# The start of an attention block with a gated feed-forward: GpSimd's order, and k of the first sequence by single tiles

## The chip, the cores and the metric

The kernel runs on one core of one Trainium2 chip. The core has five engines that run side by side and wait for each other through semaphores: PE (TensorE, matmuls, with a sequencer of its own for weight loads, PEld), DVE (VectorE), ACT (ScalarE), POOL (GpSimd) and SP (SyncE, which here only starts DMAs). DMAs are started from SP's queue or from ACT's, and sixteen DMA engines move the data.

The metric is the device time of one execution in microseconds; less is better. Three executions of the kernel before took 610.42, 611.47 and 612.76 us, so its median is 611.47 us. A further execution was profiled; it took 612.91 us.

## The reference

x has 8 sequences of 512 tokens with 256 features. Everything is float32 with a tight tolerance.

```python
xn = layernorm(x)                       # over the 256 features, eps 1e-5
# attention: 16 heads of 16, q and k rotated, a window of 250 tokens, causal
q, k, v = split(xn @ in_proj_w.T)       # in_proj_w: 768 x 256
q, k = rope(q), rope(k)
scores = (q . k) * 16 ** -0.5, masked to 0 <= t - s < 250
s = (softmax(scores) @ v) @ out_proj_w.T
# feed-forward with weights +1 or -1, from boolean matrices
h = s0 * (concat(xn, -xn) @ sign(k0))   # 512 -> 1024
h = s1 * ((2 * relu(h)) @ sign(k1))     # 1024 -> 1024
h = s2 * ((2 * relu(h)) @ sign(k2))     # 1024 -> 256
out = x + s * silu(h)
```

## The kernel before

**Tiles.** Features lie on the 128 partitions in the products: x is brought to x^T (2 chunks of 128 features by 512 tokens), and every matmul has up to 512 tokens as its columns. The feed-forward splits each activation into a high part in fp16 and a low part in fp32r (`h1h` and `h1l`, `h2h` and `h2l`) and multiplies each with its own copy of the weights (`w1h`, `w1l`); a group of 128 features is one PSUM tile `h_ps`, whose high part ACT takes out and whose low part DVE takes out after it. A PSUM tile is free for the next group only after both. Three such tiles rotate in the pool `ps_m`; the pool `ps_s` has two, which serve the first sequence's transposes, then q, then v, and later the scores.

**Order.** Nothing is scheduled by the hardware. `run` takes a list of pieces, each with a hand-written place (a number, about microseconds from the start of the first sequence's feed-forward; 42 for each sequence) and a cost, and emits them in the order of places; a piece may return follow-ups with delays in the same clock. The order in which pieces are emitted is the order in each engine's queue, and each engine works strictly through its queue. Sequence b+1 is prepared while sequence b runs, so PE has work almost all the time; the first sequence has nobody ahead of it.

**The first sequence.** Its four tiles of 128 tokens are loaded (`load_x`, L111), two from SP and two from ACT, and ACT also loads the scales `s_sb` and then the weights of k, q and v. `stats` (L245) takes mean and variance of each tile on DVE (`bn_stats`, `bn_aggr`), adds EPS (L256) and has GpSimd raise it to the power -0.5 (L257); for the first sequence this is done for two tiles at once (`n = 2`). `norm` (L309) scales a tile on DVE, `turn_x` (L315) transposes it on PE and has ACT copy it to `xT`. `project` (L375) makes k and q as two parts of 128 features, `a` and `b`; for k of the first sequence by halves of 256 tokens. Then, for k and for q alike:

- `both` multiplies the parts with cosine and sine on DVE (L404: `m_ka`, `m_kb`, `m_qa`, `m_qb`). `m_kb` and `m_qb` are one and the same buffer.
- `rotate` (L421, the work in L425) adds and subtracts them on GpSimd, two instructions of 128x512.
- `split_hi` (L439) casts the result on ACT (`kh`, `qh`; one buffer) and stores it to DRAM, `split_lo` (L445) takes the rest on DVE (L449) and stores that. q is stored twice, in two orders. `stack` (L452) loads k, q and the second q back, turned, for the scores.

`hi_after` and `lo_after` (L401) are the places of the two splits, counted from the second part's product.

**GpSimd and ACT beside it.** The weights of the second layer are made from booleans in blocks of 128 output features (`make_w1`, L188, L192 on ACT and L194 on DVE or GpSimd), placed by the list at L998: `w1l` 0 and 1 at -20 and -19 on GpSimd, `w1h` 0 and 1 at -17 and -16 on ACT. Places below zero come ahead of the first sequence's feed-forward, and so ahead of the rotations of its k and q.

Of the kernel before, what the change touches and what calls it, by code (L numbers as in the profile page):

```python
# [34 lines left out]
def tile_attention_times_gated_ffn(  # L35
# [42 lines left out]
    nc = tc.nc  # L78
    P = 128
    B, T, E = x.shape  # L80
    H = HEADS
    D = E // H
    NT = T // P
# [25 lines left out]
    xs = {}  # L109

    def load_x(b, t):  # L111
        xs[b, t] = xpool.tile([P, E], F32, tag=f"x{t}", name=f"x_{b}_{t}")
        queue = nc.scalar if b == 0 and t >= NT // 2 else nc.sync
        queue.dma_start(xs[b, t], x[b, ts(t, P), :])

    raw = ctx.enter_context(ExitStack())
    raw_pool = raw.enter_context(tc.tile_pool(name="raw", bufs=1))
    s_sb = const.tile([P, 5], F32, name="s_sb")
# [6 lines left out]
    kb2 = raw_pool.tile([P, NF1, E], U8, name="kb2")  # L125
    for t in range(NT):
        load_x(0, t)
    nc.scalar.dma_start(s_sb, s)
    for n in (1, 0, 2):
        nc.scalar.dma_start(  # L130
            wqkv_sb[:, :, ts(n, E)], w_qkv[:, ts(n, E)].rearrange("(c p) f -> p c f", p=P)
        )
# [109 lines left out]
            follow(at, g())  # L242


    def stats(b):  # L245
        st = states[b] = {}

        n = 2 if b == 0 else NT
        mv = st["mv"] = moments[:, b % 2, : 3 * NT].rearrange("p (i t) -> p t i", t=NT)
        for t in range(NT):  # L250
            bn = small.tile([P, 6], F32, tag="bn", name=f"bn_{b}_{t}")
            nc.vector.bn_stats(bn, xs[b, t])
            nc.vector.bn_aggr(mv[:, t, 1:3], bn)
            if (t + 1) % n == 0:
                part = mv[:, t + 1 - n : t + 1, 0]
                nc.vector.tensor_scalar(part, mv[:, t + 1 - n : t + 1, 2], EPS, None, ALU.add)  # L256
                nc.gpsimd.tensor_tensor(part, part, minus_half[:, :n], ALU.pow)  # L257
        if b > 0:
            enough(b)

# [48 lines left out]
    def norm(b, t):  # L309
        mv, xn = states[b]["mv"], xs[b, t]  # L310
        nc.vector.tensor_scalar(
            xn, xn, mv[:, t, 1:2], mv[:, t, 0:1], ALU.subtract, ALU.mult
        )

    def turn_x(b, t, plain=False):  # L315

        st = states[b]
        xn = xs.pop((b, t))
        if t == 0:
            st["xT"] = one.tile([P, EC, T], F32, tag="xT", name=f"xT_{b}")  # L320
            if plain:
                st["xp"] = one.tile([P, EC, T], F32, tag="xl", name=f"xp_{b}")
            else:
                for p, dt in (("h", F16), ("l", F32R)):
                    st["x" + p] = one.tile([P, EC, T], dt, tag="x" + p, name=f"x{p}_{b}")
        if not plain and t == 2:
            pt = ps_o.tile([P, T], F32, tag="po", name=f"xnT_ps_{b}_{t}")
            pt = pt[:, : EC * P].rearrange("p (c q) -> p c q", c=EC)
        elif not plain and t < 2:

            pt = ps_s.tile([P, 2, T], F32, tag="sc", name=f"xnT_ps_{b}_{t}")
            pt = pt[:, 0, : EC * P].rearrange("p (c q) -> p c q", c=EC)
        else:
            pt = ps_m.tile([P, EC, P], F32, tag="mm", name=f"xnT_ps_{b}_{t}")
        for c in range(EC):
            nc.tensor.transpose(pt[:, c, :], xn[:, ts(c, P)], ident)
        if plain:
            nc.vector.tensor_copy(st["xT"][:, :, ts(t, P)], pt)
            nc.scalar.mul(st["xp"][:, :, ts(t, P)], pt, sgnx)
            return  # L340
        hi, lo = (st["x" + p][:, :, ts(t, P)] for p in "hl")


        nc.scalar.copy(st["xT"][:, :, ts(t, P)], pt)
        st["parts", t] = [
            lambda: nc.scalar.mul(hi, pt, sgnx),
            lambda: nc.vector.scalar_tensor_tensor(lo, pt, sgnx, hi, ALU.mult, ALU.subtract),
        ]
        if t + 1 == NT:
            first_parts(0, 1)  # L350

    def first_parts(*tiles):
        for t in tiles:
            for f in states[0].pop(("parts", t)):
                f()
# [16 lines left out]
        return [(0.0, lambda: nc.scalar.copy(v_pad[:, t, :, 0:3:2, :], v))]  # L372


    def project(b, what, part, half=None):  # L375

        st = states[b]
        col = E * "qk".index(what) + P * "ab".index(part)
        if b == 0 and what == "q":
            ps = ps_s.tile([P, 2, T], F32, tag="sc", name=f"{what}{part}_ps_{b}")[:, 0]  # L380
        elif half == 1:
            ps = st.pop(part)
        else:
            ps = ps_m.tile([P, T], F32, tag="mm", name=f"{what}{part}_ps_{b}")
            st[part] = ps
        for cols in [slice(0, T)] if half is None else [ts(half, T // 2)]:
            for c in range(EC):
                nc.tensor.matmul(
                    ps[:, cols], wqkv_sb[:, c, ds(col, P)], st["xT"][:, c, cols],
                    start=(c == 0), stop=(c == EC - 1),  # L390
                )
        if half == 0:
            return

        m = turned.tile(
            [P, 2, T], F32, tag=f"m{part}", name=f"m_{what}{part}_{b}",
            bufs=2 if part == "a" else 1,
        )
        st[what, part] = m

        hi_after, lo_after = (4.0, 5.1) if b else (4.5, 5.7) if what == "k" else (5, 6.2)  # L401

        def times(i):
            nc.vector.tensor_tensor(  # L404
                m[:, i], ps, rope_sb[:, i if part == "a" else 1 - i], ALU.mult
            )

        def both():
            times(0)
            times(1)  # L410
            if part == "b":
                return [
                    (1.4, lambda: rotate(b, what)),
                    (hi_after, lambda: split_hi(b, what)),
                    (lo_after, lambda: split_lo(b, what)),
                ]


        return [(1.5 if b == 0 and what + part == "qb" else 0.0, both)]
# [40 lines left out]
    def prepare(b, plain=False):  # L460

        if b == 0 or plain:
            at = dict(stats=-40, norm=-38, x=-36, k=0, q=3, v=9.2)
            dp, dv = 1.5, 1.5
        else:

            at = dict(load=9, stats=9, down=10.5, over=12, norm=16.8, k=21.8, q=24.8, v=SEQ + 0.6)
            if b == 1:
                at.update(load=18.65, stats=15, down=18, over=18.7, norm=24.8, k=26.6, q=28.4)
            dp, dv = 1.5, 1.0  # L470
            at = {n: SEQ * (b - 1) + f for n, f in at.items()}
        out = [(at["stats"], 0, lambda: stats(b))]
        if "over" in at:
            out += [
                (at["load"], 0, lambda: load_xT(b)), (at["down"], 0, lambda: lay_down(b)),
                (at["over"], 0, lambda: lay_over(b)),
                (at["norm"], 0, lambda: norm_turned(b, 0)),
                (at["norm"] + 1.2, 0, lambda: norm_turned(b, 1)),
            ]
        for t in range(NT):  # L480
            if "over" not in at:
                out += [
                    (at["norm"] + t, 0, lambda t=t: norm(b, t)),
                    (at["x"] + t, 0.25, lambda t=t: turn_x(b, t, plain)),
                ]
            out.append((at["v"] + dv * t, 0.87, lambda t=t: project_v(b, t)))
        for what in "kq":
            for n, part in enumerate("ab"):
                if b == 0 and what == "k" and not plain:

                    out += [
                        (-34.3 if n == 0 else -32.95, 0.87, lambda p=part: project(b, "k", p, 0)),
                        (at["k"] + dp * n, 0.87, lambda p=part: project(b, "k", p, 1)),
                    ]
                else:
                    out.append((
                        at[what] + dp * n, 1.75, lambda w=what, p=part: project(b, w, p),
                    ))
        return out
# [496 lines left out]
            (-32.9 if c == 0 else -32.6, 0, lambda c=c: make_w0l(c)),  # L996
        ]
    for w, f, at, engine in (  # L998
        ("l", 0, -20, nc.gpsimd), ("l", 1, -19, nc.gpsimd), ("l", 2, 5.1, nc.gpsimd),
        ("h", 0, -17, nc.scalar), ("h", 1, -16, nc.scalar), ("h", 2, 5.2, nc.gpsimd),  # L1000
        ("l", 3, 11.8, nc.gpsimd), ("l", 4, 11.9, nc.gpsimd), ("l", 5, 12.0, nc.gpsimd),
        ("l", 6, 19.3, nc.gpsimd), ("l", 7, 19.4, nc.gpsimd), ("h", 3, 15.2, nc.scalar),
        ("h", 4, 17.0, nc.scalar), ("h", 5, 18.7, nc.scalar), ("h", 6, 20.4, nc.scalar),
        ("h", 7, 22.2, nc.scalar),
    ):
        everything.append((at, 0, lambda f=f, w=w, e=engine: make_w1(f, w, e)))
    for b in range(B):
# [4 lines left out]
        for t in range(NT):  # L1012
            if b + 1 < B:
                at = SEQ * b + 1.5 if b else 2.0
# [133 lines left out]
```

## Time and profile before

| | |
|---|---|
| median of three runs | 611.47 us |
| the profiled execution, its whole time | 612.91 us |
| its span, first to last instruction | 611.2 us |
| mean granted TensorE clock | 0.991 |
| PE busy | 596.9 us, 98% of the span |
| DVE / ACT / POOL busy | 384.2 / 295.1 / 308.0 us |

PE is the engine that sets the time. Its row is busy in all slices of the page but the first and the last, so what matters is where it stands still or runs at a lower clock. The profile gives, for each instruction, start, length and what ended the idle time before it; "[1.65 <-ACT v_pad L372]" behind an instruction says that its engine stood idle for 1.65 us until ACT's instruction at line 372 was done. `h_ps<-h1h,w1h_sb` means that the tile `h_ps` is written from `h1h` and `w1h_sb`. "PEclk" is the clock granted to TensorE as a share of full speed.

### The profile page before, as it was taken

The numbers are of one execution on the slowest core, as the hardware profiler recorded it, in microseconds if no ns is written. First come the engines' busy times: TensorE is split into PE (matmuls) and PEld (weight loads), VectorE is DVE, ScalarE is ACT, GpSimd is POOL, SyncE is SP. The second block draws the span as 40 slices with busy tenths as digits, with TensorE's granted clock in tenths as the row PEclk, the third lists the DMA queues.
The fourth block names the chain that finished last, engine by engine and source line by source line (L and its number), as shares of the span: only waits on it lengthen the run. The fifth ranks groups of instructions, "written<-read, shape, count | busy, mean of one in ns | idle before, by whom it ended". The sixth has DMA issues, their size and how long they took to land. (4 is left out here: it accounts for less than half of the span.)

```text
span 611.2 us, 11176 instructions
## 1 busy us (share of the span) xinstructions
PE 596.9 (98%) x4492; PEld 367.7 (60%) x4492; DVE 384.2 (63%) x606; ACT 295.1 (48%) x414; POOL 308.0 (50%) x368
## 2 busy tenths in 40 slices
PE   7899999999999999999999999999999999999994
PEld 5465565556665556555566566655565556667783
DVE  6654736556675584665856658566676557654774
ACT  4576654435544545545354454543554445555421
POOL 2855542346524665336634357245572446627642
PEclk9799999999999999999999999999999999999998
DMA  9371732216322263314333252432533216212201
GB/s 286 144 242 53 276 122 86 87 70 229 117 87 87 97 215 104 120 55 180 131 104 122 79 218 73 148 112 80 207 101 123 89 69 241 70 54 75 83 1 41
DMA packets 38061, 74.51 MB, mean 122 GB/s; under 512 B 5360, under 2 KB 13040, under 8 KB 38000
## 3 DMA queue, kind: packets, MB, share of 16 engines
q1 hardware_dynamic: 35568, 71.48, 34.0%
q10 hardware_dynamic: 2432, 2.23, 1.1%
q8 instruction: 37, 0.61, 0.4%
q14 instruction: 24, 0.20, 0.1%
HBM read 44.30 MB, written 29.39 MB: 121 GB/s over the span
## 5 line engine op out<-in xcount | busy, mean ns | idle before, releaser
L752 ACT ACTIVATE p<-sc 128x1024 f32<-128x1024 f32 (+2 forms) x144 | 138.3, 1013 | 75.5 <-PE sc L733 45.8
L768 POOL TENSOR_SCALAR_AFFINE_SELECT p<-p 128x512 f32<-128x512 f32 x128 | 91.1, 718 | 126.6 <-ACT p L752 126.5
L518 PE MATMUL h_ps<-h1l,w1l_sb 128*128 128x512 f32 (+1 forms) x576 | 146.2, 396 | 0.0
L518 PE MATMUL h_ps<-h1h,w1h_sb 128*128 128x512 f16 (+1 forms) x576 | 123.1, 356 | 0.0
L518 PEld LDWEIGHTS h_ps<-h1l,w1l_sb 128*128 128x128 f32 x576 | 100.2, 188 | 29.5 <-issue 9.2
L529 ACT ACTIVATE h2h<-h_ps 128x512 f16<-128x512 f32 (+1 forms) x72 | 39.5, 548 | 112.3 <-PE h_ps L518 112.3
L518 PEld LDWEIGHTS <-w1h_sb 128*128 128x128 f16 x576 | 51.2, 98 | 58.7 <-issue 17.3
L775 POOL TENSOR_SCALAR_AFFINE_SELECT p<-p 128x512 f32<-128x512 f32 (+1 forms) x96 | 49.7, 517 | 70.9 <-ACT p L752 67.4
L807 PE MATMUL po<-p,v_pad 128*32 128x378 f32 (+4 forms) x1216 | 76.7, 372 | 0.1
L633 DVE RECIPROCAL den<-den 128x256 f32<-128x256 f32 (+1 forms) x32 | 52.5, 1644 | 24.9 <-POOL den L628 24.9
L527 DVE SCALAR_TENSOR_TENSOR h2l<-h_ps,h2h 128x512 fp32r<-128x512 f32 (+1 forms) x72 | 43.7, 608 | 30.9 <-ACT h2h L529 30.9
L733 PEld LDWEIGHTS sc<-q,k 32*128 32x128 f32 x1216 | 44.0, 184 | 29.4 <-issue 21.5
L527 DVE SCALAR_TENSOR_TENSOR h1l<-h_ps,h1h 128x512 fp32r<-128x512 f32 x64 | 42.8, 680 | 29.4 <-ACT h1h L529 29.4
L884 DVE RECIPROCAL S<-S 128x128 f32<-128x128 f32 x64 | 57.5, 920 | 0.1
L733 PE MATMUL sc<-q,k 32*128 32x378 f32 (+4 forms) x1216 | 57.4, 306 | 0.1
L518 PE MATMUL h_ps<-xl,w0l_sb 128*128 128x512 f32 x128 | 53.7, 501 | 0.0
L807 PEld LDWEIGHTS po<-p,v_pad 128*32 128x32 f32 x1216 | 31.7, 109 | 28.7 <-issue 16.6
L529 ACT ACTIVATE h1h<-h_ps 128x512 f16<-128x512 f32 x64 | 38.1, 598 | 22.1 <-PE h_ps L518 22.1
L518 PE MATMUL h_ps<-xh,w0h_sb 128*128 128x512 f16 x128 | 39.8, 393 | 1.1 <-DVE h1l L527 1.1
L301 DVE TENSOR_TENSOR xT<-xT,of_all 128x512 f32<-128x512 f32 x28 | 22.7, 815 | 26.4 <-DMA of_all<-d 26.0
L572 PE MATMUL z_ps<-h2l,w2l_sb 128*128 128x512 f32 (+1 forms) x144 | 36.1, 391 | 0.2 <-DVE h2l L527 0.2
L365 PE MATMUL v_ps<-wqkv_sb,xT 128*128 128x256 f32 x128 | 33.8, 387 | 1.6 <-ACT v_pad L372 1.6
(101 smaller groups left out, 721.5 us busy)
## 6 DMA issues: line engine op xcount, KB each, us to landing
q<-dq SPq DMA_DIRECT2D x64, 256.0 KB, 3.4
dq<-qh SPq DMA_DIRECT2D x16, 512.0 KB, 3.2
dq<-m_qa SPq DMA_DIRECT2D x16, 512.0 KB, 5.5
k<-dk SPq DMA_DIRECT2D x32, 256.0 KB, 2.7
dk<-kh SPq DMA_DIRECT2D x8, 512.0 KB, 3.6
dk<-m_ka SPq DMA_DIRECT2D x8, 512.0 KB, 2.6
x<-in_x_dram SPq DMA_DIRECT2D x30, 128.0 KB, 2.8
xT<-in_x_t_dram SPq DMA_DIRECT2D x7, 512.0 KB, 5.3
```

The lines of the kernel that those rows point to most:

```text
L365: nc.tensor.matmul(v.rearrange("p n s d -> p (n s d)"), st["xT"][:, c, ts(t, P)], wqkv_sb[:, c, 2 * E :], start=(c == 0), stop=(c == EC - 1),)
L518: nc.tensor.matmul(ph, w[p][:, c, ts(f, P)], st[src + p][:, c, cols], start=(k == 0), stop=(k == n - 1),)
L527: nc.vector.scalar_tensor_tensor(lo, ph, 0.0, hi, ALU.max, ALU.subtract)
L529: high = lambda: nc.scalar.activation(hi, ph, AF.Relu)
L572: nc.tensor.matmul(pz, w2[p][:, c, ts(f, P)], st["h2" + p][:, c, cols], start=(c == 0 and p == "h"), stop=(c == NF1 - 1 and p == "l"),)
L633: nc.vector.reciprocal(part, part)
L733: nc.tensor.matmul(sc[r // 2][:, r % 2, ds(off, n)], st["k0", g][row, ts(j, P)], st[f"q{turn}", g][row, ds(j * P + first, n)], start=(turn ...
L752: nc.scalar.activation(p[:, 2 * half : 2 * half + 2, :n], sc[half][:, :, :n], AF.Exp, scale=D ** -0.5,)
L768: nc.gpsimd.affine_select(out=block, in_=block, compare_op=ALU.is_ge, fill=0.0, base=0, pattern=[[0, 4], [1, P]], channel_multiplier=-1,)
L775: nc.gpsimd.affine_select(out=block, in_=block, compare_op=ALU.is_ge, fill=0.0, base=-1, pattern=[[0, 4], [-1, beyond]], channel_multiplier=1,
L807: nc.tensor.matmul(po[32 * r : 32 * r + 32, ds(j * P + first, n)], v_columns(j, g, r), p_[:, r, ds(off, n)], start=(j == 0), stop=(done an ...
L884: nc.vector.reciprocal(part, part)
```

## The change

Four things change, all of them at the start of the kernel.

- Loads: all four tiles of x go to SP's queue, and ACT's queue begins with the weights of k; `s_sb` comes behind them.
- Statistics of the first sequence: by single tiles (`n = 1`), and `stats` itself calls `norm` of a tile once the next tile's statistics are queued.
- k of the first sequence: by tiles of 128 tokens, each right behind the transpose that it needs; the transposes have new places.
- GpSimd and ACT: `w1l` 0 and 1 move from -20 and -19 to 4.6 and 4.65, so GpSimd's queue has the rotation of k, these two blocks, the rotation of q, and then `w1l` 2 and `w1h` 2, which were ahead of q's rotation. `w1h` 1 moves on ACT from ahead of the first evacuation to behind the second (behind `kh` and `h1h` of group 1, ahead of the first copy of v). The splits have new places: the low part of k comes behind the low part `h1l` of group 1 instead of ahead of it, and the low part of q ahead of `h1l` of group 5 instead of behind it.

A branch that computes everything anew when a value is out of range uses the same functions; it isn't entered with these inputs.

```diff
     def load_x(b, t):
         xs[b, t] = xpool.tile([P, E], F32, tag=f"x{t}", name=f"x_{b}_{t}")
-        queue = nc.scalar if b == 0 and t >= NT // 2 else nc.sync
-        queue.dma_start(xs[b, t], x[b, ts(t, P), :])
+        nc.sync.dma_start(xs[b, t], x[b, ts(t, P), :])
...
-    nc.scalar.dma_start(s_sb, s)
     for n in (1, 0, 2):
+        if n == 0:
+            nc.scalar.dma_start(s_sb, s)
         nc.scalar.dma_start(
...
-    def stats(b):
+    def stats(b, plain=False):
...
-        n = 2 if b == 0 else NT
+        n = 1 if b == 0 and not plain else NT
...
                 nc.gpsimd.tensor_tensor(part, part, minus_half[:, :n], ALU.pow)
+            if n == 1 and t > 0:
+                norm(b, t - 1)
+        if n == 1:
+            norm(b, NT - 1)
...
-        for cols in [slice(0, T)] if half is None else [ts(half, T // 2)]:
+        for cols in [slice(0, T) if tile_ is None else ts(tile_, P)]:
             for c in range(EC):
                 nc.tensor.matmul(
                     ps[:, cols], wqkv_sb[:, c, ds(col, P)], st["xT"][:, c, cols],
...
-        if half == 0:
+        if tile_ is not None and tile_ + 1 < NT:
             return
...
-        hi_after, lo_after = (4.0, 5.1) if b else (4.5, 5.7) if what == "k" else (5, 6.2)
+        hi_after, lo_after = (4.0, 5.1) if b else (5.0, 6.2) if what == "k" else (4.6, 5.4)
...
-                    (at["x"] + t, 0.25, lambda t=t: turn_x(b, t, plain)),
-                ]
+                if b > 0 or plain:
+                    out.append((at["norm"] + t, 0, lambda t=t: norm(b, t)))
+                out.append((
+                    at["x"] + t if plain else (-36, -35, -34.3, -33.3)[t], 0.25,
+                    lambda t=t: turn_x(b, t, plain),
+                ))
...
-                    out += [
-                        (-34.3 if n == 0 else -32.95, 0.87, lambda p=part: project(b, "k", p, 0)),
-                        (at["k"] + dp * n, 0.87, lambda p=part: project(b, "k", p, 1)),
-                    ]
+                    for t, places in enumerate(((-35.5, -34.9), (-34.6, -33.6), (-0.9, -0.6), (0, 1.5))):
+                        out.append((
+                            places[n], 0.43, lambda p=part, t=t: project(b, "k", p, t),
+                        ))
...
-        ("l", 0, -20, nc.gpsimd), ("l", 1, -19, nc.gpsimd), ("l", 2, 5.1, nc.gpsimd),
-        ("h", 0, -17, nc.scalar), ("h", 1, -16, nc.scalar), ("h", 2, 5.2, nc.gpsimd),
+        ("l", 0, 4.6, nc.gpsimd), ("l", 1, 4.65, nc.gpsimd), ("l", 2, 10.2, nc.gpsimd),
+        ("h", 0, -17, nc.scalar), ("h", 1, 8.6, nc.scalar), ("h", 2, 10.3, nc.gpsimd),
```

More of the change, by code (lines that the diff above doesn't have):

```diff
@@ L372, in project_v, with project @@
         return [(0.0, lambda: nc.scalar.copy(v_pad[:, t, :, 0:3:2, :], v))]
-    def project(b, what, part, half=None):
+    def project(b, what, part, tile_=None):
         st = states[b]
@@ L380, in project @@
             ps = ps_s.tile([P, 2, T], F32, tag="sc", name=f"{what}{part}_ps_{b}")[:, 0]
-        elif half == 1:
-            ps = st.pop(part)
+        elif tile_:
+            ps = st[part]
         else:
@@ L471, in prepare @@
             at = {n: SEQ * (b - 1) + f for n, f in at.items()}
-        out = [(at["stats"], 0, lambda: stats(b))]
+        out = [(at["stats"], 0, lambda: stats(b, plain))]
         if "over" in at:
@@ L481, in prepare @@
             if "over" not in at:
-                out += [
-                    (at["norm"] + t, 0, lambda t=t: norm(b, t)),
-                    (at["x"] + t, 0.25, lambda t=t: turn_x(b, t, plain)),
-                ]
+                if b > 0 or plain:
[4 more added lines that the diff above has]
+                ))
             out.append((at["v"] + dv * t, 0.87, lambda t=t: project_v(b, t)))
@@ L489, in prepare @@
                 if b == 0 and what == "k" and not plain:
-                    out += [
-                        (-34.3 if n == 0 else -32.95, 0.87, lambda p=part: project(b, "k", p, 0)),
-                        (at["k"] + dp * n, 0.87, lambda p=part: project(b, "k", p, 1)),
-                    ]
+                    for t, places in enumerate(((-35.5, -34.9), (-34.6, -33.6), (-0.9, -0.6), (0, 1.5))):
+                        out.append((
+                            places[n], 0.43, lambda p=part, t=t: project(b, "k", p, t),
+                        ))
                 else:
```

## The prediction, made before the result

> **What bounds the kernel now.** I read first the list of what PE waited for, over the whole span: after its start it has four waits, and two make nearly all of it.
>
> ```profile
> PE v_ps L365 <- ACT v_pad L372: 1.6, 1, 1.6
> PE h_ps L518 <- DVE h1l L527: 1.1, 1, 1.1
> PE ka_ps L388 <- ACT xT L344: 0.5, 1, 0.5
> PE z_ps L572 <- DVE h2l L527: 0.2, 1, 0.2
> ```
>
> Then the table of stretches (us; busy time and count of each engine; granted clock):
>
> ```profile
> core 0: us, PE busy (x) PEld busy (x) DVE busy (x) ACT busy (x) POOL busy (x), PEclk, DMA share, GB/s
> ...
> 18.00:20.00 2.00, 1.93 (x9) 0.93 (x7) 0.53 (x2) 0.28 (x1) 2.00 (x3) 1.00 0.00 0
> 20.00:21.50 1.50, 0.00 (x0) 0.00 (x0) 1.50 (x3) 1.50 (x4) 1.50 (x2) 1.00 0.00 0
> 21.50:23.70 2.20, 1.13 (x4) 0.78 (x5) 2.20 (x3) 1.38 (x4) 2.20 (x2) 0.83 0.62 240
> 23.70:26.00 2.30, 2.23 (x7) 1.07 (x6) 1.21 (x3) 0.33 (x1) 2.30 (x3) 0.50 0.60 237
> 26.00:28.00 2.00, 2.00 (x6) 1.54 (x5) 0.69 (x1) 1.80 (x3) 2.00 (x3) 0.50 0.00 0
> 28.00:30.00 2.00, 2.00 (x7) 1.19 (x5) 1.97 (x2) 0.37 (x1) 1.01 (x1) 0.55 1.01 403
> ```
>
> Two gaps, then 6.83 us at half clock (22.96 to 29.79). PE works 6.02 us of these, so half of that, 3.0 us, is lost. From 46 to 603 us PE is busy 253.81 of 254 and 302.80 of 303 us: what the first 46 us gain, the end gains. Only there does the diff change orders. The timeline shows who makes the gaps (start, length, engine, line):
>
> ```profile
> 14.28 1.27 DVE L404 TENSOR_TENSOR m_kb<-kb_ps,rope_sb 128x512 f32<-128x512 f32 x2
> ...
> 14.83 2.39 POOL L194 TENSOR_SCALAR w1l_sb<-kb,sgn,sgnn 128x1024 fp32r<-128x1024 uint8 x2 [7.71 <-DMA kb<-in_k_dram]
> ...
> 17.18 2.50 POOL L425 TENSOR_TENSOR m_ka<-m_ka,m_kb 128x512 f32<-128x512 f32 x2
> ...
> 19.72 1.29 DVE L404 TENSOR_TENSOR m_qb<-qb_ps,rope_sb 128x512 f32<-128x512 f32 x2 [1.47 <-POOL m_ka L425]
> 19.72 1.04 ACT L442 CAST kh<-m_ka 128x1024 fp32r<-128x1024 f32 x1 [2.20 <-POOL m_ka L425]
> ...
> 20.84 1.20 POOL L194 TENSOR_SCALAR w1h_sb<-kb,sgn,sgnn 128x1024 f16<-128x1024 uint8 x1
> 20.92 2.19 DVE L449 TENSOR_TENSOR m_ka<-m_ka,kh 128x1024 fp32r<-128x1024 f32 x1
> 21.16 0.36 ACT L372 COPY v_pad<-v_ps 128x256 f32<-128x256 f32 x1
> ```
>
> k is ready to rotate at 15.55; GpSimd first makes two blocks of w1l. Behind the rotation wait DVE (m_qb, same buffer as m_kb) and ACT (kh, with the copy of v behind it).
>
> **The change, part by part.** Line numbers are those of before; times after are estimates.
>
> *Statistics by single tiles.* Two more additions of EPS (L256), and each tile's addition now stands in the chain: a tile with it takes 0.73 us (bn at 4.15 to bn at 4.88), without it 0.55, so +0.36. The first norm waits for its power (addition 4.27, +0.33 to GpSimd, 0.73 long: 5.33): 0.25 idle; the last waits 0.6 where 0.35 was waited before. In sum the signs start at 8.65, not 7.80. ACT's copies of x come as much later, so DVE's m_ka starts near 13.87, not 13.08: **+0.8 us on DVE**. A power of one element is not in the trace; two take 0.73, four 1.02: between 0 and 0.73, I take 0.73.
>
> *k by tiles of 128 tokens.* 32 records of 128 columns replace 16 of 256. Three of the warm-up's 128-wide records, 0.28 long, fill 0.50 us: 0.11 apart. Groups of four 256-wide ones start 0.87 apart (10.11, 10.98), 0.22 each. 32 x 0.11 = 16 x 0.22: no cost. k starts 0.6 earlier (one tile copied, not two) but then waits for tile 1's copy; the FFN starts at 15.2 instead of 15.27. I count nothing.
>
> *Loads.* Weights of k go first on ACT's queue (2.19 to 0.79). Two x tiles move to SP and push kb0 by two issues, 0.87 us. SP's wait list has kb0 landing near 7.85. Shifted by its issue it lands at 8.7; if SP's 0.75 MB, which took 7.06 us from the first issue at 0.79, become 1 MB at that rate, 2.35 later, at 10.2. It is needed at 8.47 + 0.85 = 9.3. The same 256 KB leave ACT's queue, so I take 8.7, hidden by the later statistics; the other bound costs 0.9. x tile 2 is needed at 5.7 instead of 4.88, which hides 0.87 too.
>
> *GpSimd's order.* m_kb is done at 16.35, the rotation runs 16.4 to 18.9. The wait of 1.63 is gone, less 0.8: m_qb and kh start at 18.9, **0.8 earlier**.
>
> *PE and evacuations from there.* PE's first v needs the buffer of qa, free when m_qa ends: 16.74 + 0.8 = 17.55. PE is there at 17.05: **a new wait of 0.5**. The second v waited for a copy until 21.57; by the order it now waits for m_qb (20.2), and PE arrives then: that gap is gone. ACT does kh to 19.9, h1h of block 1 to 20.5, then the w1h block that moved here (1.23), v's copy, h1h of block 2 to 22.4. DVE does m_qb, h1l of block 1 (to 21.2), the low part of k from 21.1, then h1l of block 2. PE's group 4 starts at 21.25; group 5 needs that last one.
>
> The low part of k (L449) takes 1.23 to 2.19 us in this trace. The 2.19 has a w1h block under way for its first 1.1 us, and the excess, 0.97, is about that; now a w1l block ends 0.15 us after its start, so I take 1.35. [...]
>
> Low part done 22.45, h1l 23.1, group 5 at 23.15: **a wait of 1.0 from 22.15** (1.9 with the long bound). No wait shows for the next: three groups of 0.91 and two v of 0.86 bring PE to 27.6. The second layer's first group needs the buffer freed by h1l of block 5, which the change queues behind q's low part: rotation of q held by k's low part until 22.4, done 24.85; qh to 25.9; low part to 27.3; h1l 27.9: **a wait of 0.35**. It starts at 27.95; before, 32.00.
>
> *q's way through DRAM.* Scores follow 7.3 us later, at 35.25, and need q's second turned copy 0.27 after. Its issue stood 4.5 us behind the last store of q's low part (30.5 to 35.0). The store now goes at 27.65, the issue at 32.15; q loads land in 2.7 to 3.7 us here: 34.9 to 35.9. But the stores of q's high part, 1 MB at 0.4 MB/us (403 GB/s above), are now 1.3 and not 2.9 us ahead, which can cost up to 1.6 more. The wait is 0 to 2.0; **I take 0.7**.
>
> *Clock.* PE's idle of 2.7 in the 3.84 us from 19.93 came before half clock; the next longest, 0.46, before none. The new gap of 1.0 lies nearer the latter: full clock.
>
> **Sum.** 32.00 - 27.95 = 4.05, less 0.7: 3.35 us. As losses: before 1.65 + 1.06 + 3.0 and some 0.3 of restarts, 6.0; after 0.5 + 0.1 + 1.0 + 0.35 + 0.7, 2.65. The profiled execution took 612.91 (span 611.2): 609.6. It lies 1.44 above the median of the runs, 611.47, on which the same would be 608.1. I can't tell whether that is the profile or the moment at which its clock fell; I take the middle, **608.8**, and write the rivals on that scale (before: 612.2).
>
> **Rivals.**
> - *The new gap halves the clock too.* For it: 1.0 to 1.9 us is longer than any gap that went unpunished. Against: one gap, not two. Half of the 3.0, up to all of it, comes back, less the waits that it hides (0.35 + 0.7): 609.3 to 610.8. Chance 0.2.
> - *The half clock isn't due to these gaps.* For it: it began 1.4 us after the first ended. Against: it occurs nowhere else until the end. Then 3.0 stays: 3.35 - 3.0, 611.8. [...] Chance 0.03.
> - *More is gained.* DVE's delay of 0.8 is counted from dependent steps; if it is hidden and q's loads are in time, the 0.5 and 0.7 go, and part of the 1.0: 606.5 to 607.5. Chance 0.2.
> - *Slower: kb0 comes late.* SP now has 256 KB more ahead of it. If these pass at half the rate above, 4.7 us, kb0 lands at 12.55, 3.2 after it is needed; the FFN's first weights, DVE, m_ka and the first v slip by 3.2, the wait there is as long as the two that halved the clock, and the 3.0 is lost as well: 608.8 + 3.2 + 3.0 = 615.0. It decides from 1.4 us of delay on, where the first v's wait of 0.5 becomes 1.9, about what PE idled up to the fall of the clock. Against: kb0 is still issued ahead of rope and kb1. Chance 0.09.
>
> **How the numbers follow.** My forecast holds 0.48. Its own range is 607.7 (no wait for q, half of the clock's scatter) to 610 (kb0 at its other bound). The range to 80%: 606.6, into the third rival, to 611.6, through the first; the last stays out. A measurement of this kernel can tell 0.5%, 3.06 us, from nothing: faster means under 608.4, slower over 614.5. Of my forecast half lies under 608.4 (0.25), with the 0.2 of the third rival and 0.01 of the first: 0.46. Slower: 0.07 of the last. The rest, 0.47, is within.
>
> **What would show it.** In the changed profile GpSimd should rotate k from 16.4 with no w1l block before; m_qb and kh start near 18.9; PE waits 0.5 for the first v on m_qa, about 1 us for group 5 on h1l, little for the second v; the clock is 1.00 through 46 us; the second layer starts near 28. The step on the clock is wrong if PEclk falls under 0.9 in any slice between 20 and 32, the one on statistics if the signs start before 8.3 or after 9, the one on loads if DVE waits for kb0. I am wrong altogether if the second layer starts after 31.

## The result, and the profile after

| | before | after |
|---|---|---|
| median | 611.18 us (10 runs, 610.07 to 612.76) | 609.01 us (10 runs, 608.51 to 610.09) |
| ratio, with its 95% interval | | 0.9968 (0.9959 to 0.9977) |
| profiled execution: time, span, mean clock | 612.91, 611.2, 0.991 | 609.12, 607.4, 0.997 |

The changed kernel is 2.17 us faster at the median, 0.3%. Between the two profiled executions it is 3.79 us; why these differ is the first thing that the experiments had to tell.

What PE waited for over the whole span after the change (us in total, times, the longest), its first wait left out:

```profile
PE sc L739 <- DMA q<-dq: 1.2, 2, 0.9
PE ka_ps L392 <- ACT xT L348: 0.5, 1, 0.5
PE h_ps L524 <- DVE h1l L533: 0.3, 1, 0.3
PE v_ps L369 <- DVE m_qa L408: 0.2, 1, 0.2
PE z_ps L578 <- DVE h2l L533: 0.2, 1, 0.2
```

The two long waits of before (1.6 for a copy of v, 1.1 for `h1l`) are gone. In their place stand two short ones and, new, 1.2 us for q's loads. The table of stretches, same columns as before:

```profile
core 0: us, PE busy (x) PEld busy (x) DVE busy (x) ACT busy (x) POOL busy (x), PEclk, DMA share, GB/s
...
20.00:21.50 1.50, 1.50 (x9) 1.09 (x8) 1.50 (x2) 1.50 (x3) 1.50 (x2) 1.00 0.80 314
21.50:23.70 2.20, 1.91 (x9) 1.31 (x8) 2.14 (x4) 1.60 (x4) 2.20 (x2) 1.00 0.53 212
23.70:26.00 2.30, 2.30 (x12) 1.49 (x12) 0.80 (x2) 1.76 (x4) 2.30 (x3) 1.00 0.12 48
```

From 20 to 21.5 us PE was idle before; now it is busy all the time, and in the two rows behind it PEclk stays at 1.00, where it was 0.83 and 0.50. The timeline after (start, length, engine, line, operation; in brackets the idle time and what ended it):

```profile
15.87 2.52 POOL L429 TENSOR_TENSOR m_ka<-m_ka,m_kb 128x512 f32<-128x512 f32 x2 [7.56 <-DVE m_kb L408]
...
17.64 1.13 PE L369 MATMUL v_ps<-wqkv_sb,xT 128*128 128x256 f32 x4 [0.24 <-DVE m_qa L408]
18.37 2.39 POOL L194 TENSOR_SCALAR w1l_sb<-kb,sgn,sgnn 128x1024 fp32r<-128x1024 uint8 x2
18.42 1.29 DVE L408 TENSOR_TENSOR m_qb<-qb_ps,rope_sb 128x512 f32<-128x512 f32 x2 [0.24 <-POOL m_ka L429]
...
20.41 1.02 PE L369 MATMUL v_ps<-wqkv_sb,xT 128*128 128x256 f32 x4
20.60 1.22 DVE L453 TENSOR_TENSOR m_ka<-m_ka,kh 128x1024 fp32r<-128x1024 f32 x1
20.71 3.50 POOL L429 TENSOR_TENSOR m_qa<-m_qa,m_qb 128x512 f32<-128x512 f32 x2
...
22.63 0.59 PE L524 MATMUL h_ps<-xh,w0h_sb 128*128 128x512 f16 x2 [0.29 <-DVE h1l L533]
...
35.84 0.62 PE L739 MATMUL sc<-q,k 32*128 32x378 f32 x12 [0.88 <-DMA q<-dq]
```

k is rotated first, and the two w1l blocks follow at 18.37. The second product of v (20.41) shows no wait. The second layer starts at 27.22 us (before 32.00), 4.78 earlier. PE's last product ends only 3.35 earlier: q's loads take back 0.88 and 0.31, and the small rest has no single row.

### The profile page after: what moved, and what is told of

Its sections match the earlier page's. It is cut to its first block, busy times and chain, and to the rows that moved or that the text cites. A ratio compares the mean times of both kernels' runs of the same rounds, so it can differ in the third digit from the quotient of the medians.

```text
span 607.4 us, 11212 instructions
## 1 busy us (share of the span) xinstructions
PE 594.8 (98%) x4508; PEld 367.2 (60%) x4508; DVE 383.9 (63%) x608; ACT 294.9 (49%) x414; POOL 312.0 (51%) x370
## 5 line engine op out<-in xcount | busy, mean ns | idle before, releaser
L774 POOL TENSOR_SCALAR_AFFINE_SELECT p<-p 128x512 f32<-128x512 f32 x128 | 92.8, 731 | 126.0 <-ACT p L758 125.9
L524 PE MATMUL h_ps<-xl,w0l_sb 128*128 128x512 f32 x128 | 52.3, 489 | 0.0
L535 ACT ACTIVATE h1h<-h_ps 128x512 f16<-128x512 f32 x64 | 38.1, 598 | 18.9 <-PE h_ps L524 18.9
L524 PE MATMUL h_ps<-xh,w0h_sb 128*128 128x512 f16 x128 | 38.4, 382 | 0.3 <-DVE h1l L533 0.3
L429 POOL TENSOR_TENSOR m_ka<-m_ka,m_kb 128x512 f32<-128x512 f32 x16 | 20.1, 1275 | 28.1 <-DVE m_kb L408 28.1
```

Of the source, the lines that this page charges most:

```text
L524: nc.tensor.matmul(ph, w[p][:, c, ts(f, P)], st[src + p][:, c, cols], start=(k == 0), stop=(k == n - 1),)
L535: high = lambda: nc.scalar.activation(hi, ph, AF.Relu)
L774: nc.gpsimd.affine_select(out=block, in_=block, compare_op=ALU.is_ge, fill=0.0, base=0, pattern=[[0, 4], [1, P]], channel_multiplier=-1,)
```

## The experiments

Twelve kernels ran, each beside the kernel before on the same chip. "Base" says what the edit starts from.

| run | base and edit | median, us | ratio to before (95%) |
|---|---|---|---|
| (changed kernel) | | 609.01 | 0.9968 (0.9959 to 0.9977) |
| e0_before_again | before, unchanged | 611.65 | 0.9997 (0.9983 to 1.0011) |
| e1_order_only | before + new order | 608.18 | 0.9943 (0.9924 to 0.9962) |
| e2_head_only | before + loads, statistics, tiles | 610.27 | 0.9977 (0.9965 to 0.9988) |
| e3_filled_gaps | before + 14 and 9 fillers | 613.91 | 1.0036 (1.0021 to 1.0050) |
| e5_filled_right | before + 7 and 4 fillers, shorter warm-up | 611.88 | 1.0008 (0.9995 to 1.0021) |
| e6_order_and_loads | e1 + new loads | 609.90 | 0.9970 (0.9957 to 0.9982) |
| e7_pairs | changed, statistics by pairs | 611.22 | 0.9989 (0.9975 to 1.0004) |
| e8_q_first | e1, q rotated ahead of w1l 0, 1 | 608.06 | 0.9937 (0.9922 to 0.9952) |
| e9_old_loads | changed, old loads | 609.73 | 0.9972 (0.9961 to 0.9984) |
| e10_x_two_queues | e9, weights of k ahead of scales | 610.03 | 0.9978 (0.9968 to 0.9988) |
| e11_act_clear | e8, ACT and DVE reordered | 607.73 | 0.9939 (0.9926 to 0.9952) |
| e12_less_gpsimd | e11, one block from GpSimd to ACT | 607.24 | 0.9933 (0.9918 to 0.9947) |

### The kernel before once more

No edit.

> The kernel before, unchanged, so that the clock of each of its runs can be read. The profiled execution took 612.91 us at a mean clock of 0.991, above all ten runs of the kernel before (610.07 to 612.76), while all ten of the changed kernel have 0.997 or 0.998. Theory: every run of the kernel before has the half clock (6.83 us of it are 0.0055 of the span, so a clock of 0.991 to 0.992), and what differs from run to run is when it falls and how much of PE's work lies under it, 1.5 to 3.0 us of loss; the median lies near 611.2. Rival: only some runs have it; then the runs fall into two groups, one at 0.997 and some 3 us shorter than the other at 0.991.

The rival was nearer. Of the 96 runs of the kernel before whose clock was read in the four comparisons (12 of them under this label), 39 have 0.997 or 0.998 and a median of 610.64 us; 45 have 0.995 or less and a median of 612.06; the 12 at 0.996 lie between, at 611.62. Only 9 are at 0.991, like the profiled one, with 612.69. There are no two clean groups. In the profiles of this kernel the half clock lasts one stretch of 3.41 us (this run's) or two (6.83 us, the profile taken before the change), which take 0.003 or 0.006 off the mean. The mean also holds the end of each run: behind PE's last product the record falls to half for the last 1.99 to 4.97 us of the span (this run's profile and e7's), another 0.002 to 0.004. By these figures 0.997 and 0.998 mean no stretch at half clock before it and 0.995 or less at least one, while 0.996 can be either. This run's profile, at 0.996, has one (the columns are those of the table of stretches above):

```profile
21.00:24.40 3.40, 1.53 (x7) 1.06 (x7) 3.40 (x5) 3.09 (x6) 3.40 (x3) 1.00 0.44 172
24.40:27.80 3.40, 3.40 (x9) 2.19 (x8) 1.43 (x3) 1.55 (x3) 3.40 (x3) 0.50 0.37 143
27.80:30.00 2.20, 2.20 (x11) 1.40 (x10) 1.58 (x2) 1.55 (x4) 2.20 (x3) 0.99 0.59 236
```

PE is busy 1.53 of the first 3.40 us; the next 3.40 run at half clock, and then it is over. So the median of all 96 runs (611.50) lies 0.86 us above that of the runs without half clock. This is an estimate of what the half clock costs at the median, and a high one if the runs without it also have the shorter gaps, which their times alone can't tell. The profile taken before the change was of the rare, costlier kind; its kind lies 1.19 above the median of all, which accounts for most of the 1.62 by which the profiles differ more than the medians.

### The order alone, the head alone

Of the change, e1_order_only has these lines alone; e2_head_only is the changed kernel with these lines as they were before:

```diff
-        hi_after, lo_after = (4.0, 5.1) if b else (4.5, 5.7) if what == "k" else (5, 6.2)
+        hi_after, lo_after = (4.0, 5.1) if b else (5.0, 6.2) if what == "k" else (4.6, 5.4)
...
-        ("l", 0, -20, nc.gpsimd), ("l", 1, -19, nc.gpsimd), ("l", 2, 5.1, nc.gpsimd),
-        ("h", 0, -17, nc.scalar), ("h", 1, -16, nc.scalar), ("h", 2, 5.2, nc.gpsimd),
+        ("l", 0, 4.6, nc.gpsimd), ("l", 1, 4.65, nc.gpsimd), ("l", 2, 10.2, nc.gpsimd),
+        ("h", 0, -17, nc.scalar), ("h", 1, 8.6, nc.scalar), ("h", 2, 10.3, nc.gpsimd),
```

> The kernel before with the new places of w1l, w1h and the two splits alone; loads, statistics and k as before. My account: all of the gain is the order's, and the new head costs 0.8 us on DVE. So m_ka starts at 13.08 (changed kernel 13.90), GpSimd rotates k from 15.05 to 17.57, m_qb and kh start near 17.6; the changed kernel's waits of 0.24 us for the first v and 0.29 us for group 5 go, the feed-forward starts 0.14 earlier, the second layer at 26.5 (27.22); the wait for q stays near 0.9. Clock 0.997, time 608.3 us (607.9 to 608.7). Rival A, the head's 0.8 us are hidden: 609.0, as the changed kernel. Rival B, the single tiles bring the gain: near 611.

> The changed kernel with the old places of w1l, w1h and the splits: the new loads, statistics and tiles of k alone. My account: they shift DVE and GpSimd by 0.8 us and gain nothing, so k's rotation starts near 18.0 (before 17.18), m_qb and kh near 20.5 (19.72), the gap before the second v grows from 1.65 to about 2.4 us, the clock falls to half as before (0.991), second layer near 32.8, time near 612.0 us (611.2 to 612.8). Rival: the single tiles gain by themselves: under 610.5, with a clock of 0.997.

The order alone gives 608.18 us, inside the forecast, and is 0.83 below the changed kernel's median. So the order brings all of the gain. That the new head gives part of it back is likely and not settled: the intervals of the two ratios just touch, and five of its six runs lie below the changed kernel's 608.65, the second fastest of ten; but in the two profiles PE's last product ends at nearly the same time (599.90 and 599.97), e1's profiled run being the slowest of its six. In its profile k is rotated from 15.37, m_qb and kh start at 17.9, neither the wait for the first v nor that for group 5 is over 0.1, and the scores wait 1.09 us for q.

The head alone was misjudged: 610.27, not 612. Its gap before the second v is 0.51 us, not 2.4. In the old order GpSimd's first w1l block waits for its DMA, until 14.83 before and 15.02 here, and m_qb and kh start at 19.72 and 19.92: the head hardly moves that end of the gap. The other end is later in this profile, since the feed-forward starts at 16.09 instead of 15.27. Most of that is this run's own: the changed kernel, with the same head, starts its feed-forward at 15.42, and its clock first rose at 6.14 us, here at 8.16. The clock is kept more often: 9 of the 12 runs have 0.997 or 0.998, against 39 of 96 of the kernel before. Against those 39 (610.64) 0.4 us is left.

### Filling the gaps

e3_filled_gaps has one line more than before:

```diff
+        (10.65, 0, lambda: warm(14)), (10.9, 0, lambda: warm(9)),
```

e5_filled_right has warm(7) and warm(4) in it, and its edit also cuts the warm-up at the start of PE's queue from nine products to four, which its expectation doesn't mention:

```diff
-        (-34.6, 0, signs), (-40.5, 0, lambda: warm(9)), (-34.7, 0, lambda: warm(0)),
+        (-34.6, 0, signs), (-40.5, 0, lambda: warm(4)), (-34.7, 0, lambda: warm(0)),
+        (10.65, 0, lambda: warm(7)), (10.9, 0, lambda: warm(4)),
```

> The kernel before with 14 products of 128x128 that nobody reads in PE's queue ahead of the second v and 9 ahead of the group after it; at 0.11 us each they fill the two gaps of 1.65 and 1.06 us and shorten neither. Theory, PE's idle time makes the half clock: it is 1.00 through 46 us, the second layer starts near 29.1 us instead of 32.0. Then the scores come near 36.7, where q's second copy lands at 37.7 to 38.7, so 1 to 2 of the 3 us become a wait for q: 609.2 to 610.2 us on the scale of the median, clock 0.997. Rival, the half clock has another cause (it comes a fixed time after something else): it stays, second layer at 32 to 32.2, time 611.2 or a little more, clock 0.991.

> The fillers of before again, at the right length: one 128x128 product makes two records 0.11 us apart, so the 14 and 9 products of the earlier run lasted 3.12 and 2.01 us and pushed the work behind them back by themselves. Now 7 and 4 products, 1.56 and 0.89 us for gaps of 1.65 and 1.06. Theory, PE's idle time makes the half clock: no run shows a clock under 0.996 (a few under 0.997 for a late start at half clock), against 17 of 41 runs of the kernel before at 0.995 or less; the time is that of those runs of before that have 0.997 or 0.998, 610.8 us, with some 0.2 on top: 610.6 to 611.2, and no run over 612.2. Rival, idle time isn't the cause: clocks down to 0.991 in a third of the runs, median 611.5 or more.

On the clock both agree with the theory: of 24 runs none lies under 0.996, where 45 of 96 of the kernel before do (8 of the 24 are at 0.996, which leaves a single stretch open). On the time both missed. The first was mis-made, as the second expectation says. The second was too, by the shorter warm-up, as its timeline of PE shows:

```profile
2.75 2.07 PE L224 MATMUL warm<-ident 128*128 128x128 f32 x8 [2.75 <-POOL ident masks.py:199]
6.68 1.12 PE L336 MATMUL xnT_ps<-ident,x 128*128 128x128 f32 x4 [1.86 <-DVE x L311]
...
22.23 1.73 PE L224 MATMUL warm<-ident 128*128 128x128 f32 x14
23.79 1.03 PE L365 MATMUL v_ps<-wqkv_sb,xT 128*128 128x256 f32 x4
```

The warm-up has 8 records instead of 18. PE then idles 1.86 us ahead of the first transpose, the clock first rises at 12.46 (before 5.90), and the feed-forward starts at 17.74 (15.27). PE reaches the place of the first gap at 22.23, when kh had been started 2.05 us earlier; before, the gap had ended 1.86 after kh. There was no gap left, and the 14 filler records cost their full 1.56 us. The gap of the kernel before is slack for a late start, and its length changes from run to run. So both runs speak for PE's idle time as the cause of the half clock, and neither gives its price; fillers of the right length with the full warm-up were not run. A second sign of the cause comes from e6 below, where a wait at another place brings the half clock too.

### The parts of the head

e6_order_and_loads adds the new loads to e1:

```diff
-        queue = nc.scalar if b == 0 and t >= NT // 2 else nc.sync
-        queue.dma_start(xs[b, t], x[b, ts(t, P), :])
+        nc.sync.dma_start(xs[b, t], x[b, ts(t, P), :])
...
-    nc.scalar.dma_start(s_sb, s)
     for n in (1, 0, 2):
+        if n == 0:
+            nc.scalar.dma_start(s_sb, s)
```

e7_pairs takes the single-tile statistics out of the changed kernel:

```diff
-        n = 1 if b == 0 and not plain else NT
+        n = 2 if b == 0 else NT
...
-                if b > 0 or plain:
-                    out.append((at["norm"] + t, 0, lambda t=t: norm(b, t)))
+                out.append((at["norm"] + t, 0, lambda t=t: norm(b, t)))
```

e9_old_loads is the changed kernel with the loads of before (e6's diff undone), e10_x_two_queues the same with its second half kept:

```diff
-    nc.scalar.dma_start(s_sb, s)
     for n in (1, 0, 2):
+        if n == 0:
+            nc.scalar.dma_start(s_sb, s)
```

> The run with the new order alone (608.18 us), plus the new loads: x from SP's queue, the weights of k first on ACT's. Theory: with the old loads PE's first product of k waits in some runs for its weights (1.23 and 1.46 us in two of three profiles of the old loads, at 8.9 and 9.3 instead of 7.8); with the new ones it never does, so the first k comes by 8.2 and the runs scatter less: 607.5 to 608.1 us. Rival: x tiles 2 and 3, later by 0.87 us on SP, delay the statistics of the second pair, and this costs as much or more: 608.3 to 609.0.

> The changed kernel with its statistics by pairs again, as before; loads, k by single tiles and the order stay. Theory: the single-tile statistics are what delays DVE by 0.8 us, so m_ka starts near 13.2 instead of 13.90, the waits for the first v and for group 5 (0.24 and 0.29 us) go, and the time is about that of the new order alone, 608.2 us (607.8 to 608.6), against 609.01. Rival: the tiles of k, not the statistics, cost the 0.8 between the new order alone and the changed kernel: 609.0, with m_ka near 13.9.

> The changed kernel with the loads of before: x tiles 2 and 3 and then the scales from ACT's queue, the weights of k behind them. The new loads on the new order alone cost 1.7 us with statistics by pairs (609.90 against 608.18: the statistics of tile 3 start at 6.82 instead of 5.33), and the single-tile statistics bring that back (611.22 to 609.01). Theory: the new loads are the cost also under single-tile statistics: tile 3's statistics start near 5.7 instead of 6.74, the signs near 7.7 instead of 8.67, m_ka near 13.1 to 13.4 instead of 13.90: 607.9 to 608.5 us. Rival: loading the weights of k first is worth more than x's lateness costs, since with the old loads they landed only at 8.9 and 9.3 in two profiles of six: 609.0 to 609.8.

> As the run before, but on ACT's queue the weights of k stand ahead of the scales (behind x tiles 2 and 3). Theory: x early and the weights 0.5 us earlier than before's, so few runs wait for them: 607.5 to 608.1 us, 0.2 to 0.5 less than with the old loads. Rival: the place of the scales' issue changes nothing: equal to the run before within 0.2.

My account held in none of the four: e9 came out as its rival had it, e6 and e7 worse than both theories, e10 0.3 above e9. The new loads on the new order cost 1.7 us (608.18 to 609.90 in e6; no run of one reaches into the range of the other). The timeline of e6, DVE and PE:

```profile
6.83 0.43 DVE L252 BATCH_NORM_STATS2 bn<-x 128x6 f32<-128x256 f32 x1 [0.90 <-DMA x<-in_x_dram]
...
7.58 0.73 DVE L311 TENSOR_SCALAR x<-x,moments 128x256 f32<-128x256 f32 x2
...
8.05 0.76 PE L336 MATMUL xnT_ps<-ident,x 128*128 128x128 f32 x4 [1.30 <-DVE x L311]
```

With statistics by pairs no tile is scaled before all four are in. Tile 3 arrives later on SP's queue (its statistics start at 6.83; 5.34 with the old loads), the first scaling slips from 6.06 to 7.58, and PE stands still for 1.30 us. In that run's profile PE is then idle for 52% of a stretch of 3.41 us, and the next one runs at half clock.

The single-tile statistics cure just this. The changed kernel scales its first tile at 5.17 with the same loads, and its tile 3 takes its statistics at 6.75 without holding anybody up. Without them (e7) the median is 611.22 instead of 609.01. What the single tiles lose without the new loads can be read in PE's row of e9:

```profile
8.52 0.68 PE L392 MATMUL ka_ps<-xT,wqkv_sb 128*128 128x128 f32 x4 [1.13 <-DMA wqkv_sb<-in_w_qkv_dram]
9.04 0.38 PE L340 MATMUL xnT_ps<-ident,x 128*128 128x128 f32 x2
```

The first product of k waits 1.13 us for its weights, which now load behind x and the scales, and the transpose of tile 1 (L340) stands behind that product in PE's queue. All later tiles are pushed back: k's last copy ends at 11.89 instead of 10.70, m_ka starts at 15.09 instead of 13.90. Not all of these 1.19 us are the weights': the copy that the product also needs ends at 7.80, so the weights hold it for some 0.7 (to 8.52), and the rest comes with this run's start, whose clock first rose at 8.10 instead of 6.14 (its first two transposes begin at 6.76 and take 0.63 us, in the changed kernel 6.47 and 0.38). Moving the scales' issue (e10) leaves that wait at 1.01 us, and the time the same within its scatter. So the new loads lose with the old statistics: e6 is clear of e1, and e7's median is 2.21 above the changed kernel's, its interval just touching. That the single tiles lose with the old loads rests on this profile and on medians 0.72 us apart: the ratios of e9 and the changed kernel, 0.9972 and 0.9968, overlap almost wholly. On the new order the old head is by its median still 0.83 us better. What the products of k by tiles cost by themselves was not separated: e7 against e6 (611.22 against 609.90) differs in them, but the runs of e7 scatter from 609.81 to 613.52.

### What is left: q's way, ACT and GpSimd

e8_q_first, from e1:

```diff
-        ("l", 0, 4.6, nc.gpsimd), ("l", 1, 4.65, nc.gpsimd), ("l", 2, 10.2, nc.gpsimd),
+        ("l", 0, 10.1, nc.gpsimd), ("l", 1, 10.15, nc.gpsimd), ("l", 2, 10.2, nc.gpsimd),
```

e11_act_clear, from e8:

```diff
-        hi_after, lo_after = (4.0, 5.1) if b else (5.0, 6.2) if what == "k" else (4.6, 5.4)
+        hi_after, lo_after = (4.0, 5.1) if b else (5.0, 8.0) if what == "k" else (4.6, 5.4)
...
-        ("h", 0, -17, nc.scalar), ("h", 1, 8.6, nc.scalar), ("h", 2, 10.3, nc.gpsimd),
+        ("h", 0, -17, nc.scalar), ("h", 1, 15.1, nc.scalar), ("h", 2, 10.3, nc.gpsimd),
```

e12_less_gpsimd, from e11:

```diff
-        ("h", 0, -17, nc.scalar), ("h", 1, 15.1, nc.scalar), ("h", 2, 10.3, nc.gpsimd),
+        ("h", 0, -17, nc.scalar), ("h", 1, 15.1, nc.scalar), ("h", 2, 15.15, nc.scalar),
```

> The new order alone (608.18 us) with w1l 0 and 1 behind q's rotation too. Theory: what is left is q's way through DRAM (the scores wait 1.09 us for it, then 0.18). GpSimd rotates q right behind k, from about 18.6 instead of 20.2; qh then is set by its place on ACT behind group 4 and by the store of kh from the same buffer, near 23.1 instead of 23.7; q's stores and loads come 0.6 earlier: 607.4 to 607.8 us. Rival: the two blocks of w1l come too late for DVE and PE or lock the low part of k, or the loads of q wait for something else: 608.2 or more.

> The run with q's rotation ahead of w1l 0 and 1 (608.06 us), plus: block 1 of w1h moves on ACT from 8.6 to 15.1, behind the feed-forward's first layer, and the low part of k goes behind group 2's low part. There the low part of k ran beside q's rotation and took 2.20 us instead of 1.23, so group 5 waited 0.93 us. Theory: group 2's copy on ACT then starts near 19.9 instead of 20.8, its low part on DVE near 20.5, group 5 doesn't wait, qh and q's low part come some 0.4 earlier, the second layer starts near 26.6 instead of 27.46, the scores' wait for q grows from 0.13 to about 0.6: 607.3 to 607.8 us. Rival: q's way through DRAM ends no earlier, so all of the 0.9 becomes a wait of the scores: 608.0 to 608.3.

> The fastest run so far (607.73 us) with block 2 of w1h made by ACT, behind blocks 1 and 3's place (15.15), and not by GpSimd. In that run's profile no wait is left in the feed-forward's first layer, and the longest one is new: the product of the softmax with v waits 0.86 us at 39.27 for GpSimd's masks, which stand behind its blocks of weights (the last ends at 38.84). Theory: with one block of 1.20 us fewer, the first mask starts near 37.7, the 0.86 go, ACT's evacuation of the second layer's first group is some 0.3 late, which nobody waits for: 606.8 to 607.3 us. Rival: the gain is given back to the wait for q's loads or to ACT: 607.5 to 608.0.

e8 did to q what was expected (qh at 22.64 instead of 23.75, the wait for q 0.13 instead of 1.09) and gained nothing (608.06), since an equal wait came up elsewhere in its timeline:

```profile
18.80 2.51 POOL L425 TENSOR_TENSOR m_qa<-m_qa,m_qb 128x512 f32<-128x512 f32 x2 [0.82 <-DVE m_qb L404]
...
20.19 2.20 DVE L449 TENSOR_TENSOR m_ka<-m_ka,kh 128x1024 fp32r<-128x1024 f32 x1
...
23.04 0.59 PE L518 MATMUL h_ps<-xh,w0h_sb 128*128 128x512 f16 x2 [0.93 <-DVE h1l L527]
```

The low part of k starts while GpSimd is in q's rotation and takes 2.20 us, where e1's took 1.23; the `h1l` behind it is late, and group 5 waits 0.93. e11 takes the low part out of that place and a block of weights out of ACT's way. Its first layer has no wait, the second layer starts at 26.68 (27.46), and the median is 607.73. Its timeline shows what is next:

```profile
37.68 1.21 POOL L194 TENSOR_SCALAR w1l_sb<-kb,sgn,sgnn 128x1024 fp32r<-128x1024 uint8 x1
...
38.84 0.66 POOL L768 TENSOR_SCALAR_AFFINE_SELECT p<-p 128x512 f32<-128x512 f32 x1
...
40.14 1.07 PE L807 MATMUL po<-p,v_pad 128*32 128x378 f32 x16 [0.86 <-POOL p L775]
```

GpSimd's own blocks of weights now hold the first mask, and PE's product with v waits for it. With one block fewer (e12) the mask starts at 37.43 and that wait is gone. The scores wait again for q:

```profile
34.76 0.62 PE L733 MATMUL sc<-q,k 32*128 32x378 f32 x12 [0.77 <-DMA q<-dq]
...
37.43 0.65 POOL L768 TENSOR_SCALAR_AFFINE_SELECT p<-p 128x512 f32<-128x512 f32 x1
```

607.24 us (606.88 to 607.87) is the fastest of all, 0.9933 of before against the changed kernel's 0.9968; the two intervals don't overlap. Those of e1, e8, e11 and e12 all overlap, so none of these steps by itself is settled on the time; the traces show where the wait went. What e12 still loses at its start is the old loads' price: in its profile PE waits 0.8 us for the weights of k.

## Why the prediction came out as it did

The forecast was 608.8 us, the measured median 609.01, in the case that was held the likeliest. Step by step:

- *Statistics.* Signs at 8.65 forecast, 8.67 measured; m_ka 13.87 and 13.90. Right. A power of one element takes 0.58 to 0.66 us; 0.73 was taken. With the old loads the signs come at 8.51 (e9), so it is the statistics that delay them, as counted.
- *k by tiles.* The records are 0.11 apart as counted; the feed-forward starts at 15.42 (15.2 forecast, 15.27 before). A cost of nothing is not contradicted in this profile; by itself the part stays open (e7).
- *Loads.* "Hidden by the later statistics" holds for kb0: DVE makes w0h at 9.34 without waiting. But the step looked only at kb0 and x tile 2. It did not see that the weights of k, loaded late, stop PE's first product of k in some runs of before (e0_before_again: 1.23 us), nor that the new loads without single-tile statistics cost 1.7 us (e6). The profile before could not show it, as its weights came in time.
- *GpSimd's order.* Rotation from 15.87 (16.4 forecast; GpSimd needs only the first half of m_kb, whose second runs to 16.38), m_qb and kh at 18.42 (18.9). The right mechanism, 0.5 better than counted.
- *The waits.* First v 0.24 (0.5), second v none (little), group 5 0.29 (1.0), second layer none (0.35), start 27.22 (27.95). All smaller, by 1.3 us together. The low part of k took 1.22 us; 1.35 was taken. The first instruction of q's rotation, begun 0.11 us after it, took 2.26 us (elsewhere 1.28), so the hold that the sum has for this rotation is there: done at 24.21 (24.85). In the profile before it is 2.24 for the same instruction beside that low part, and e8 shows the same the other way round: the rotation had begun first, and the low part took 2.20 instead of e1's 1.23. Why the two hold each other up no run shows.
- *q's way.* 1.2 us of waiting against 0.7, within the bounds of 0 to 2.0. The errors, of the waits and of what came behind them, cancel: PE's end came 3.35 us earlier, exactly the sum's 3.35, and the whole span 3.8. That the sum came out exactly is luck.
- *Clock.* Full after the change, as forecast, in all ten runs. The mis-sized term is the one before it: "half of that, 3.0 us, is lost" is true of the profiled execution alone. Over the runs of the kernel before it costs some 0.86 us at the median, because more than a third of them haven't got it. The text left open whether the profile's 1.44 us above the median was the profile or the clock, and took the middle. Most of it was the clock, as the nine runs at 0.991 lie 1.19 above the median of the 96; the gain at the median is 2.17, not 3.35. On the median's scale the sum gave 608.1, and the middle of the two scales, not a better reading, brought 608.8 near: that is luck too.
- *The rivals.* That the new gap halves the clock, that the half clock has another cause, and that kb0 comes late did not occur. "More is gained" counted on DVE's 0.8 us being hidden; it isn't: m_ka is at 13.40 in the order alone and at 13.90 here, and without the new head the median is 0.83 us lower.

## What to carry to other kernels

Read the clock of several executions before pricing a clock loss from one profile: here the profiled execution had the rare, long form of it. A gap on the bounding engine is also slack for whatever is late ahead of it; once a change closes the gap, earlier delays count, so parts that looked free (loads, statistics) have to be costed again in the new order. And when one wait goes, look who shares the queue that was reordered: here a wait of 0.9 to 1.1 us came back at q's loads (e1), then at DVE's low part (e8), then at GpSimd's masks (e11), and the medians fell by only 0.1 to 0.5 us from each run to the next.

## What the runs showed of the hardware

The clock record of each profile changes only at steps of 3.41 us, whose phase differs from run to run (the clock first rises at 5.90, 6.14, 7.35, 7.47 us in four profiles). From the first rise to the fall at the end, its stretches last 17.07, 6.83 and 576.85 us before the change, which are 5, 2 and 169 such steps, and 597.33 us after it, which are 175. Laying such steps over PE's instructions gives the idle share of each step and the clock granted in the next:

```
clock    PE idle in a step of 3.41 us                  clock in the next step
full     52%, 55%, 56%                                 half
full     39%, 38%, 36%, 31%, 27%, 26%, 23% and less    full
full     end of run: 62%, 70%, 72%, 76% and more       half
full     end of run: 56%, 53%, 44%, 42%, 36% and less  full
half     21%, 14% (three), 12% (two), 8% and less      full
half     22%, 23%, 24%, 29%, 39%, 42%, 43% and more    half
```

The rows are of all 14 profiles. Steps ahead of the first record are laid back from it, and their clock shows in the warm-up's records, 0.21 us apart at half clock and 0.11 at full; "end of run" are the step in which PE's last product ends and those behind it. In these profiles no step idle for 44% or less halved the clock, and every one idle for 62% or more did. In between both occur: 52% (e6), 55% (e0) and 56% (before) halved it, while at the end of e12 and e0 steps of 53 and 56% were followed by one more at full clock. So the idle share alone, as read here, doesn't fix the bound, and what else counts stays open. The clock came back after steps idle for 21% or less, and not after those of 22% or more.

The prediction's threshold, a length of a single gap, was the wrong measure: 1.84 and 0.09 us of idle time, nearly all in one step, were enough (e0_before_again), 1.23 us in one step was not (36%), and in the profile before the second gap of 1.06 us did not start the half clock but kept it for a second step (24%).
